# Attention weights turned in four tiles with another column order, a second score taken ahead, butterfly adds split over two engines, and PSUM pools in another order

## The chip, the cores and the metric

The kernel runs on one core of a Trainium2 chip. The core has five engines that work side by side, each through its own list of instructions in order: TensorE (PE, matrix products; its weight loads are shown apart as PEld), VectorE (DVE), ScalarE (ACT), GpSimd (POOL) and SyncE (SP, which here only issues DMA transfers). They meet through semaphores. The metric is the time of one execution on the device in microseconds (us); lower is better.

## The reference, cut to what matters

Everything is float32. The input is two images of 128 channels and 64 x 64 points. Layer 0 is a neighbourhood attention with its projections. Layer 1 takes the 4096 points of an image as tokens of 128 channels: a self-attention in which a token doesn't see itself, and then a "ffn" that filters along the tokens (a spectral convolution). The change is in layer 1.

```python
def _L1_attn_ref(q):                    # q: (2, 4096, 128), normalized tokens
    sim = jnp.einsum('blh,bmh->blm', q, q) * scale
    sim = jnp.where(diag[None, :, :], jnp.float32(-1000000000.0), sim)
    attn = jax.nn.softmax(sim, axis=-1)
    return jnp.einsum('blm,bmh->blh', attn, q)
...
x = x + _L0_conv_ref(_gn(x), ...)       # layer 0
t = _to_tokens(x)
t = t + _L1_attn_ref(_ln_t(t))          # layer 1: attention
t = t + _L1_ffn_ref(_ln_t(t), ...)      # layer 1: spectral filters
```

The filters are long convolutions over the tokens plus products with three short lags; the kernel computes the long ones with block transforms.

## The kernel before, in words

**Scores once for each pair.** Queries and keys are the same tokens, so the matrix of scores is symmetric. The 4096 tokens of an image are cut into 8 chunks of 512, and `attention(b, fill)` goes through the 36 pairs `(a, c)` with `c >= a`. For a pair and each of the four tiles `k` of 128 tokens of `a`, `weights` multiplies (L926; L935 for the diagonal pair `a == c` and for the pair (6, 7)) a tile of `a` with the 512 tokens of `c` into a PSUM `bank`, and ACT writes `exp` of it to SBUF, `e` (L931; L942 for the others). Four of them make the half `eh` of 128 x 2048.

**Each weight used twice.** `e` as it stands gives what the tokens of `a` add to the output of chunk `c`: four products `other <- e, tok` (L1056), summed in one PSUM bank, `other`, which DVE then adds to the output `xa` (L1065; L1067 is the copy for the first row). `other` has one buffer, so the next pair's first product waits until DVE has read it. Turned around, `e` gives what the tokens of `c` add to chunk `a`: products `own <- et, tok` (L984) into a bank that gathers a whole row `a`, added to `xa` at its end (L989, L991).

**Turning.** For pairs that are neither diagonal nor (6, 7) (`far`), `sent` writes `eh` to DRAM (`eb`, issued by ACT, L958), `moved` fetches it into `et` with the blocks of 32 rows exchanged (four DMAs from SP, L965), and `turned` turns the 32 x 32 blocks in place on DVE (L974). The other pairs are turned on PE (L948, L980, with copies L949 and L981 on DVE); in a diagonal pair DVE also masks the diagonal (L940), and tile `k` takes its columns left of the diagonal from the `exp` of earlier tiles, turned by PE. `MOVE, TURN, DELAY = 2, 7, 8` say how many steps after sending the fetch, the turning and the products are written down; one pair has four steps `j`. `pass_on(2)` puts up to two due turned products in the list, before the first `other` product of a pair and after each other one.

**What sets the order.** The inner loop writes for each step: one score of the following pair, due turned products, the product into `other`, and a piece of other work from `fill()`. That work comes from `filler`: layer norms and transforms of finished chunks (`after`), filters, weights of the ffn. In the beginning of the first image's attention a scheduler orders the instructions; from L1046 on the order is as written for PE, DVE, ACT, POOL and SP.

**The transforms' butterflies.** `after` ends with `store`: ACT copies a transform from PSUM to `uo` (L1156), and an addition and a subtraction of its halves go to `ub` (L1160), which is then sent to DRAM (`us`). `uo` has 2 buffers and `ub` 4. The engine is `adder[0]`: GpSimd in the attention, and DVE from the end of the second image's attention on (L1538). Then the DMAs to `us` are issued by SP (L1107), before that by GpSimd (L1091).

**The passage to the ffn.** After the attention the last chunks' `after` and the short lags (`short_lags`, products L1219, added to `xa` on DVE by L1235) remain. Then the attention's PSUM pools are closed, and the ffn opens its own: `ps_c` with four banks `pc` for the first products (L1597, copied to `y` by L1602), and `ps_p` with the sums `acc0` to `acc3` (L1616). The last short lags use these sums' banks too. The ffn fills the span's last 760 us, in an order written by hand for PE.

Of the kernel before, what the change touches and what calls it, by code (L numbers as in the profile page):

```python
# [9 lines left out]
AF = mybir.ActivationFunctionType  # L10
ALU = mybir.AluOpType
AX = mybir.AxisListType
PSUM = bass.MemoryType.PSUM

P = 128
# [13 lines left out]
ASCALE = P ** -0.5  # L29
# [73 lines left out]
def kernel(  # L103
# [16 lines left out]
    nc = tc.nc  # L120
# [18 lines left out]
    tt, tok, cm = [None, None], [None, None], [None, None]  # L139
# [6 lines left out]
    space = tok[0].rearrange("p n c -> p (n c)")  # L146
# [93 lines left out]
    with l0a:  # L240
# [64 lines left out]
        flat = rpb_pad.rearrange("h r w -> (h r w)")  # L305
# [384 lines left out]
        halves = [4 * c for c in CHUNKS]  # L690
# [101 lines left out]
        for k, (b, g) in enumerate(order):  # L792
            t = {}
# [83 lines left out]
    with ap_:  # L877
# [23 lines left out]
        def attention(b, fill):  # L901
# [11 lines left out]
            far = lambda a, c: a != c and (a, c) != (6, 7)  # L913
            chunk = lambda a: slice(CHUNKS[a] * 512, (CHUNKS[a] + 1) * 512)

            def weights(a, c, k, left, halves):

                n = 4 * CHUNKS[a] + k
                lo = k * P if a == c else 0
                ps = bank()  # L920
                if k == 0:
                    halves.append(ep.tile([P, 2048], F32, tag="e", name="e"))
                eh = halves[0]
                keys = cm[b][:, chunk(c)]
                if far(a, c):
                    nc.tensor.matmul(  # L926
                        ps.rearrange("p (q t j) -> p q t j", q=4, t=4), lhsT=cm[b][:, n * P : (n + 1) * P],
                        rhs=keys.rearrange("p (t q j) -> p q t j", t=4, q=4), start=True, stop=True,
                    )
                    e = eh.rearrange("p (q k r) -> p k q r", q=4, k=4)[:, k]  # L930
                    nc.scalar.activation(  # L931
                        e, ps.rearrange("p (q r) -> p q r", q=4), AF.Exp, bias=0.0, scale=ASCALE
                    )
                    return e
                nc.tensor.matmul(  # L935
                    ps[:, lo:], lhsT=cm[b][:, n * P : (n + 1) * P], rhs=keys[:, lo:], start=True, stop=True
                )
                if a == c:
                    ks = slice(k * P, (k + 1) * P)
                    nc.vector.tensor_tensor(ps[:, ks], ps[:, ks], ndiag, ALU.add)  # L940
                e = eh[:, k * 512 : (k + 1) * 512]
                nc.scalar.activation(  # L942
                    e[:, lo:], ps[:, lo:], AF.Exp, bias=0.0, scale=ASCALE
                )
                if lo:
                    pt = bank()
                    for j in range(k):
                        nc.tensor.transpose(pt[:, j * P : (j + 1) * P], left[j][:, lo : lo + P], ident)  # L948
                    nc.vector.tensor_copy(e[:, 0:lo], pt[:, 0:lo])  # L949
                return e  # L950

            def in_place(ins):
                return ins if ordered else tc.keep_in_program_order(ins)
# [15 lines left out]

            def turned(et):  # L970

                for q in (0, 2):
                    flat = et[:, q : q + 2].rearrange("p q r -> p (q r)")
                    in_place(nc.vector.transpose(flat, flat))  # L974

            def turned_here(et, es, m):

# [16 lines left out]
            def pair_onto(own, a, c, et, t):  # L994
                if (a, c) == (6, 7):
                    onto(own, 4 * CHUNKS[c] + t, own, et[:, t], False, t == 3)
                    if t == 3:
                        complete(a, own)
                    return
                onto(  # L1000
                    own, 4 * CHUNKS[c] + t, own.rearrange("p (k q i) -> p q k i", k=4, q=4),
                    et.rearrange("p q (k t i) -> p t q k i", k=4, t=4)[:, t], False, c == 7 and t == 3,
                )
                if (c, t) == (7, 3):
                    complete(a, own)

            coming_, late, turns, ordered, owns = [], [], [], [], {}
            step = 0

            def coming_of(a, c, k, left, halves):  # L1010

                e = weights(a, c, k, left, halves)
                if far(a, c) and k == 3:
                    coming_.append((step, sent(halves[0]), a, c))
                return e
# [16 lines left out]
            es, halves = [], []  # L1032
# [4 lines left out]
            for i, (a, c) in enumerate(pairs):  # L1037
                following = pairs[i + 1] if i + 1 < len(pairs) else None
                coming, halves = [], []
                if a != c:  # L1040
                    other = ps_o.tile([P, 512], F32, tag="other", name="other")
                else:
                    owns[a] = ps_o.tile([P, 512], F32, tag="own", name="own", bufs=2)
                for j in range(4):
                    if tt[1] is not None and not ordered:
                        ordered.append(written.enter_context(tc.manual_schedule(engines={engines.PE, engines.DVE, engines.Activation, engines.Pool, engines.SP})))  # L1046
                    if following:
                        coming.append(coming_of(*following, j, coming, halves))
                    n = 4 * CHUNKS[a] + j
                    turn = lambda v, o: v.rearrange(o, q=4) if far(a, c) else v  # L1050
                    if j == 0:
                        pass_on(2)
                    if a == c:
                        onto(owns[a], n, owns[a], es[j], j == 0, a == 7 and j == 3)
                    else:
                        nc.tensor.matmul(  # L1056
                            turn(other, "p (q r) -> p q r"), lhsT=tok[b][:, n, :], rhs=es[j],
                            start=(j == 0), stop=(j == 3),
                        )
                    if a != c and j == 3:  # L1060
                        xs, ov = xa[b][:, chunk(c)], other
                        if far(a, c):
                            xs, ov = xs.rearrange("p (t q j) -> p q t j", t=4, q=4), ov.rearrange("p (q t j) -> p q t j", q=4, t=4)
                        if a:
                            nc.vector.tensor_tensor(xs, ov, xs, ALU.add)  # L1065
                        else:
                            nc.vector.tensor_copy(xs, ov)  # L1067
                    if a != c and not far(a, c):
                        if j == 0:
                            here = ep.tile([P, 4, 512], F32, tag="et", name="et", bufs=2)  # L1070
                        turned_here(here, es, j)
                        late.append((step + 1, a, c, here, j))
                    if j:
                        pass_on(2)
                    fill()
                    step += 1
                es = coming
# [5 lines left out]
            written.close()  # L1083


        adder = [nc.gpsimd]
        queued_, turns_, crowd_ = [], [0, 0], [[]]

        def send_one():
# [26 lines left out]
        def after(b, c):  # L1116
# [35 lines left out]
            def store(pu, n, r0, m, ri):  # L1152

                for s in range(2):
                    both = sp.tile([P, 512], F32, tag="uo", name="uo", bufs=2)
                    nc.scalar.copy(both[:, 0 : 2 * n], pu[s][:, 0 : 2 * n])  # L1156
                    room()
                    ub = sp.tile([P, 2, 256], F32, tag="ub", name="ub", bufs=4)
                    for sgn, op in enumerate((ALU.add, ALU.subtract)):
                        adder[0].tensor_tensor(ub[:, sgn, 0:n], both[:, 0:n], both[:, n : 2 * n], op)  # L1160
                    to = us[b, par, r0 : r0 + m, :, :, 2 * hh + s, 2 * fp : 2 * fp + 2]
                    if ri is not None:
                        fresh(to[:, :, ri].rearrange("k g f d -> k g (f d)"), ub)
                        continue
                    for sgn in range(2):
                        for f in range(2):
                            fresh(to[:, sgn, :, f].rearrange("k i d -> i k d"), ub[64 * f : 64 * f + 64, sgn, 0:P])
# [17 lines left out]
            for e in range(2):  # L1185
                for f in range(2):
                    for s in range(2):
# [3 lines left out]
                            rhs=z[rows_, 2 * e + f, :], start=True, stop=True,  # L1191
# [343 lines left out]
        kept = []  # L1535
        fill, left = filler(1, steps, kept, slow)
        attention(1, fill)
        adder[:] = [nc.vector]  # L1538
        stores_left()
        crowd_[0] = None  # L1540
        for gen in (*steps, slow):
# [25 lines left out]
    outf = out.rearrange("b c h w -> b c (h w)")  # L1567
    with ExitStack() as cv:
        cp = cv.enter_context(tc.tile_pool(name="conv", bufs=5))
        ps_c = cv.enter_context(tc.tile_pool(name="ps_c", bufs=4, space=PSUM))  # L1570
        ps_p = cv.enter_context(tc.tile_pool(name="ps_p", bufs=1, space=PSUM))
        used = [0]

        def slot():
# [195 lines left out]
        b = NB - 1  # L1770
# [117 lines left out]
```

## Time and profile before

| | |
|---|---|
| median of 3 runs | 1981.72 us (1977.47 to 1988.21) |
| the profiled execution | 1969.95 us, its span from first to last instruction 1968.2 us |
| mean granted clock of TensorE | 0.992 |
| DVE transposes L974, 128x1024 | 108, mean 1220 ns |
| products L1056 (`other`), L984 (`own`, turned), L926 (scores), records | 448 of 595 ns, 448 of 596 ns, 432 of 599 ns |
| ACT `exp` L931, 128x512 | 216, mean 599 ns |
| butterflies L1160, 128x256 | 108 on POOL, mean 734 ns; on DVE median 418 ns over both sizes |

How to read it: the profile is of one execution on the chip. A row of the groups names line, engine, operation, what is written and read, the shape, the count, then busy time and mean length, then the idle time of the engine just before and who ended it. The ends of matmuls are modelled, so two that follow each other overlap in the record. Stages by time: layer 0 until about 350, attention of the first image to 750, of the second to 1145 (work of the neighbouring stages is mixed into each), the passage to 1210, the ffn to the end.

### The profile page before, as it was taken

The numbers are of one execution on the slowest core, as the hardware profiler recorded it, in microseconds if no ns is written. First come the engines' busy times: TensorE is split into PE (matmuls) and PEld (weight loads), VectorE is DVE, ScalarE is ACT, GpSimd is POOL, SyncE is SP. The second block draws the span as 40 slices with busy tenths as digits, with TensorE's granted clock in tenths as the row PEclk, the third lists the DMA queues.
The fourth block names the chain that finished last, engine by engine and source line by source line (L and its number), as shares of the span: only waits on it lengthen the run. The fifth ranks groups of instructions, "written<-read, shape, count | busy, mean of one in ns | idle before, by whom it ended". The sixth has DMA issues, their size and how long they took to land.

```text
span 1968.2 us, 50791 instructions
## 1 busy us (share of the span) xinstructions
PE 1897.2 (96%) x20504; PEld 1346.5 (68%) x20504; DVE 950.2 (48%) x2934; ACT 732.6 (37%) x1718; POOL 725.6 (37%) x1193
## 2 busy tenths in 40 slices
PE   6899998999999999999999998999999999999998
PEld 4577776444444444444444446999998999999987
DVE  5799997454554534354544374333333343333332
ACT  3789987323233333232332213222222222222221
POOL 4366886514633335533424420222221122222211
PEclk9999999999999999999999999999999999999999
DMA  5222221757766544988866413222222223222211
GB/s 155 63 62 61 62 61 39 178 158 227 219 185 191 151 121 126 260 214 231 242 191 184 126 46 84 69 66 68 66 66 54 58 74 86 67 66 68 67 39 44
DMA packets 249768, 226.14 MB, mean 115 GB/s; under 512 B 126815, under 2 KB 204655, under 8 KB 242112
## 3 DMA queue, kind: packets, MB, share of 16 engines
q1 hardware_dynamic: 222786, 129.15, 27.3%
q10 hardware_dynamic: 8126, 58.04, 7.6%
q0 software_dynamic: 18624, 35.72, 6.3%
q8 instruction: 163, 2.67, 0.6%
q14 instruction: 69, 0.57, 0.1%
HBM read 131.40 MB, written 91.25 MB: 113 GB/s over the span
## 4 chain that ended last, share of the span: by engine, by line
PE 82%; DVE 8%; POOL 4%; DMA 2%; issue 1%; ACT 1%; SPq 1%; ACTq 0%; DVEq 0%; POOLq 0%
PE acc L1616 28%; PE own L984 12%; PE bank L926 8%; PE other L1056 8%; PE pc L1597 7%; PE bank L349 2%; PE bank L935 2%; PE bank L559 2%; PE bank L1219 2%; PE bank L1175 2%; PE bank L202 2%; DVE et L974 1%; PE bank L523 1%; PE pc L1655 1%; PE po L581 1%
## 5 line engine op out<-in xcount | busy, mean ns | idle before, releaser
L1602 DVE COPY y<-pc 128x512 f32<-128x512 f32 x320 | 206.0, 685 | 346.7 <-PE pc L1597 346.4
L1616 PE MATMUL acc<-y,mpl 32*128 32x256 f32 x5120 | 323.1, 380 | 0.8 <-DVE af L1626 0.8
L1602 ACT COPY y<-pc 128x512 f32<-128x512 f32 x320 | 171.8, 589 | 393.3 <-PE pc L1597 388.1
L1616 PE MATMUL acc<-y,mmi 32*128 32x256 f32 x5120 | 315.1, 375 | 0.0
L1616 PEld LDWEIGHTS acc<-y,mpl 32*128 32x128 f32 x5120 | 289.0, 186 | 7.6 <-DVE af L1626 1.6
L1616 PEld LDWEIGHTS acc<-y,mmi 32*128 32x128 f32 x5120 | 290.7, 185 | 2.9
L1627 POOL TENSOR_TENSOR af<-af 128x512 f32<-128x512 f32 x39 | 49.8, 1276 | 597.5 <-DVE af L1626 597.5
L1056 PE MATMUL other<-e,tok 128*128 128x512 f32 x448 | 230.1, 595 | 6.8 <-DVE xa L1065 6.8
L931 ACT ACTIVATE e<-bank 128x512 f32<-128x512 f32 x216 | 129.2, 599 | 271.5 <-PE bank L926 264.4
L926 PE MATMUL bank<-cm 128*128 128x512 f32 x432 | 223.6, 599 | 0.0
L984 PE MATMUL own<-et,tok 128*128 128x512 f32 x448 | 212.1, 596 | 9.1 <-DVE et L974 4.7
L1597 PE MATMUL pc<-ct,ut 32*128 32x256 f32 x2560 | 210.1, 377 | 2.0 <-DVE y L1602 2.0
L1597 PEld LDWEIGHTS pc<-ct,ut 32*128 32x128 f32 x2560 | 171.5, 186 | 8.3 <-DVE y L1602 3.8
L984 PEld LDWEIGHTS own<-et,tok 128*128 128x128 f32 x448 | 83.2, 190 | 118.3 <-issue 93.7
L1160 POOL TENSOR_TENSOR ub<-uo 128x256 f32<-128x256 f32 (+1 forms) x160 | 99.2, 656 | 172.3 <-ACT uo L1156 153.6
L974 DVE STREAM_TRANSPOSE et<-et 128x1024 f32<-128x1024 f32 x108 | 127.7, 1220 | 57.6 <-DMA et<-eb 57.6
L1056 PEld LDWEIGHTS other<-e,tok 128*128 128x128 f32 x448 | 81.0, 190 | 100.5 <-issue 82.4
L926 PEld LDWEIGHTS bank<-cm 128*128 128x128 f32 x432 | 75.7, 190 | 72.8 <-issue 66.5
L546 ACT ACTIVATE p<-p,mn 128x196 f32<-128x196 f32 x256 | 114.4, 449 | 13.1 <-DVE mn L536 12.5
L1091 POOL DMA_DIRECT2D us<-ub x158 | 107.8, 723 | 11.5 <-DMA us<-ub 8.5
L1156 ACT COPY uo<-bank 128x512 f32<-128x512 f32 (+1 forms) x96 | 45.4, 517 | 98.3 <-PE bank L1175 57.8
L174 POOL TENSOR_TENSOR ln_rs<-ln_rs,mhalf 128x4 f32<-128x4 f32 x24 | 24.7, 1030 | 147.3 <-DVE ln_rs L173 147.3
(267 smaller groups left out, 2635.9 us busy)
## 6 DMA issues: line engine op xcount, KB each, us to landing
eb<-e ACTq DMA_DIRECT2D x54, 1024.0 KB
et<-eb SPq DMA_DIRECT2D x216, 256.0 KB
ut<-us SPq DMA_DIRECT2D x156, 128.0 KB
us<-ub POOLq DMA_DIRECT2D x54, 256.0 KB, 4.7
vw<-vd SPq DMA_DIRECT2D x256, 49.0 KB
ct<-gs SPq DMA_DIRECT2D x312, 40.0 KB
ct<-gs SPq DMA_DIRECT2D x312, 32.0 KB
vd<-v SPq DMA_DIRECT2D x128, 32.0 KB
```

The source lines that it names most:

```text
L546: nc.scalar.activation(p, p, AF.Exp, bias=t[name + "mn"][:, h : h + 1], scale=-1.0, accum_out=t["den"][:, u, h : h + 1],)
L926: nc.tensor.matmul(ps.rearrange("p (q t j) -> p q t j", q=4, t=4), lhsT=cm[b][:, n * P : (n + 1) * P], rhs=keys.rearrange("p (t q j) -> p ...
L931: nc.scalar.activation(e, ps.rearrange("p (q r) -> p q r", q=4), AF.Exp, bias=0.0, scale=ASCALE)
L974: in_place(nc.vector.transpose(flat, flat))
L984: nc.tensor.matmul(out_, lhsT=tok[b][:, n, :], rhs=e, start=first, stop=last, skip_group_check=True)
L1056: nc.tensor.matmul(turn(other, "p (q r) -> p q r"), lhsT=tok[b][:, n, :], rhs=es[j], start=(j == 0), stop=(j == 3),)
L1091: by.dma_start(out=to, in_=part)
L1160: adder[0].tensor_tensor(ub[:, sgn, 0:n], both[:, 0:n], both[:, n : 2 * n], op)
L1597: nc.tensor.matmul(pcs[j].rearrange("p (g o c) -> p o g c", g=4, o=2)[:, :, at], lhsT=ut[rows_, par, :], rhs=cv_[rows_], start=True, stop= ...
L1602: (nc.scalar.copy if j % 2 else nc.vector.tensor_copy)(y[:, :, :, 4 * kl + j, :], pcs[j].rearrange("p (g x k) -> p k g x", g=4, k=KF))
L1616: nc.tensor.matmul(acc[j][:, 0:256], lhsT=(mmi if l else mpl)[rows_, k, :], rhs=y[rows_, k, 2 * l : 2 * l + 2].rearrange("p s n x -> p (s ...
L1627: eng.tensor_tensor(af[:, 0:2], af[:, 0:2], af[:, 2:4], ALU.add)
```

## The change

Four parts:

1. `turned` makes four transposes, each of one tile `t` (4 x 128 columns of `et`), instead of two of 1024 columns in a row. For that the order of columns inside `eh` changes from (q, k, t, j) to (q, t, k, j), where `q` is the block of 32 rows, `k` the tile of `a`, `t` the tile of `c` and `j` the column in a block: ACT writes `e` so, `other` is read and written so, and `pair_onto` reads `et` so.
2. At the first step of a pair, if the pair isn't diagonal and no turned product is due, two scores of the following pair are put in the list instead of one; the second step then has none.
3. After the second image's attention only the subtractions of the butterflies go to DVE; the additions stay on GpSimd.
4. In the ffn the pool of the sums is opened before that of the first products, so that the sums get the first four banks.

```diff
-                    e = eh.rearrange("p (q k r) -> p k q r", q=4, k=4)[:, k]
+                    e = eh.rearrange("p (q t k j) -> p k q t j", q=4, t=4, k=4)[:, k]
                     nc.scalar.activation(
-                        e, ps.rearrange("p (q r) -> p q r", q=4), AF.Exp, bias=0.0, scale=ASCALE
+                        e, ps.rearrange("p (q t j) -> p q t j", q=4, t=4), AF.Exp, bias=0.0, scale=ASCALE
                     )
...
-                for q in (0, 2):
-                    flat = et[:, q : q + 2].rearrange("p q r -> p (q r)")
-                    in_place(nc.vector.transpose(flat, flat))
+                for t in range(4):
+                    part = et[:, :, t * P : (t + 1) * P]
+                    in_place(nc.vector.transpose(part, part))
...
-                    et.rearrange("p q (k t i) -> p t q k i", k=4, t=4)[:, t], False, c == 7 and t == 3,
+                    et.rearrange("p q (t k i) -> p t q k i", k=4, t=4)[:, t], False, c == 7 and t == 3,
...
-                    if following:
-                        coming.append(coming_of(*following, j, coming, halves))
+                    due = late and late[0][0] <= step
+                    while following and len(coming) < min(4, j + (2 if j == 0 and a != c and not due else 1)):
+                        coming.append(coming_of(*following, len(coming), coming, halves))
                     n = 4 * CHUNKS[a] + j
-                    turn = lambda v, o: v.rearrange(o, q=4) if far(a, c) else v
+                    turn = lambda v, o: v.rearrange(o, q=4, t=4) if far(a, c) else v
...
-                            turn(other, "p (q r) -> p q r"), lhsT=tok[b][:, n, :], rhs=es[j],
+                            turn(other, "p (q t j) -> p q t j"), lhsT=tok[b][:, n, :], rhs=es[j],
...
-        adder = [nc.gpsimd]
+        adder = [nc.gpsimd, nc.gpsimd]
...
                     for sgn, op in enumerate((ALU.add, ALU.subtract)):
-                        adder[0].tensor_tensor(ub[:, sgn, 0:n], both[:, 0:n], both[:, n : 2 * n], op)
+                        adder[sgn].tensor_tensor(ub[:, sgn, 0:n], both[:, 0:n], both[:, n : 2 * n], op)
...
         attention(1, fill)
-        adder[:] = [nc.vector]
+        adder[1] = nc.vector
...
+        ps_p = cv.enter_context(tc.tile_pool(name="ps_p", bufs=1, space=PSUM))
         ps_c = cv.enter_context(tc.tile_pool(name="ps_c", bufs=4, space=PSUM))
-        ps_p = cv.enter_context(tc.tile_pool(name="ps_p", bufs=1, space=PSUM))
```

## The prediction

> **What bounds the kernel now.** I read the page first, then the stretches of the span, then who TensorE waits for, and last the timeline around single waits.
>
> The page's first part, busy time by engine:
>
> ```profile
> span 1968.2 us, 50791 instructions
> ...
> PE 1897.2 (96%) x20504; PEld 1346.5 (68%) x20504; DVE 950.2 (48%) x2934; ACT 732.6 (37%) x1718; POOL 725.6 (37%) x1193
> ```
>
> TensorE (PE) is busy 96% of the span, so a change that gives it no less work can win only what it idles: 71 us in all. The stretches (length, then busy time of PE, PEld, DVE, ACT, POOL, granted clock, DMA share, GB/s) say how much of that lies where the diff reaches:
>
> ```profile
> 350.00:1150.00 800.00, 782.17 (x2507) 368.19 (x2506) 367.25 (x904) 245.25 (x463) 328.98 (x493) 1.00 0.66 184
> ...
> 1192.00:1194.00 2.00, 0.00 (x0) 0.00 (x0) 2.00 (x9) 0.00 (x0) 0.00 (x0) 1.00 0.47 149
> 1194.00:1198.00 4.00, 3.75 (x6) 1.50 (x6) 0.11 (x1) 0.00 (x0) 0.00 (x0) 0.65 0.14 43
> ```
>
> The two attention passes (350 to 1150) leave PE idle 17.8 us. DVE is 46% busy there (367.25 of 800). After it comes a hole before the first sums product at 1194, and a lower clock after it. What ends PE's waits in the attention (total, times, longest):
>
> ```profile
> PE other L1056 <- DVE xa L1065: 6.8, 10, 1.7
> PE own L984 <- DVE et L974: 4.7, 7, 1.0
> PE own L984 <- DVE et L981: 2.8, 2, 1.4
> ...
> PE own L984 <- POOL ub L1160: 1.0, 1, 1.0
> ...
> PE own L984 <- POOL tt L1507: 0.2, 1, 0.2
> ```
>
> Two kinds carry it: a product into `own` that waits for turned weights, and a first product into `other` that waits until DVE has read that bank. One of each in the timeline (start, length, what, and in brackets the idle time before):
>
> ```profile
> 580.80 2.36 DVE L974 STREAM_TRANSPOSE et<-et 128x1024 f32<-128x1024 f32 x2
> ...
> 581.62 1.02 PE L1056 MATMUL other<-e,tok 128*128 128x512 f32 x2
> ...
> 583.22 1.99 PE L984 MATMUL own<-et,tok 128*128 128x512 f32 x4 [0.57 <-DVE et L974]
> ```
>
> ```profile
> 1003.74 0.68 DVE L1065 TENSOR_TENSOR xa<-other,xa 128x512 f32<-128x512 f32 x1
> ...
> 1004.48 1.12 PE L1056 MATMUL other<-e,tok 128*128 128x512 f32 x2 [0.91 <-DVE xa L1065]
> ```
>
> One product is two matmul records (448 records for 224 products), 0.43 us apart from start to start and 0.59 long, so a product takes 0.86 us and a bracket of g means that PE is g + 0.16 us late.
>
> [...] and the row says 1220:
>
> ```profile
> L974 DVE STREAM_TRANSPOSE et<-et 128x1024 f32<-128x1024 f32 x108 | 127.7, 1220 | 57.6 <-DMA et<-eb 57.6
> ```
>
> [...] in the one place where the two share the butterfly of `uo` (four DVE adds beside GpSimd's, against four alone: 0.69 us more):
>
> ```profile
> 1149.12 2.12 DVE L1160 TENSOR_TENSOR ub<-uo 128x256 f32<-128x256 f32 x4 [3.17 <-ACT uo L1156]
> ...
> 1174.35 1.43 DVE L1160 TENSOR_TENSOR ub<-uo 128x256 f32<-128x256 f32 x4 [0.59 <-ACT uo L1156]
> ```
>
> [...] The stretch 1194 to 1198 shows it (0.65 granted) after 2.8 us of idleness.
>
> **The change, part by part**, against the profiled execution (span 1968.2, 1969.95 with what lies around it).
>
> *Turning tile by tile.* Before, two transposes cover all four tiles, so tile 0 is ready after 2.36 us. In the built program of the changed kernel each of the 216 `own` products waits for its own transpose. [...] bounds are half of the old one (0.61) and, if the four pieces of 128 columns cost as much as the whole did, 1.22. I take 0.69: tile 0 is ready 1.67 us earlier, tile 1 0.69 later, while PE needs 0.86 for a product. The nine waits of this kind (4.7 + 1.0 + 0.2 us idle, 0.99 the longest; the last two releasers are mere neighbours of a late L974) are 5.9 + 9 x 0.16 = 7.3 us of lateness, and three that show no idle time come 0.25 late: 8.1 us. All are shorter than 1.67, so all go. On DVE the four take 2.76 against 2.36 to 2.44, up to 0.4 us for each of 54 turns, 21 us at most: DVE has 433 idle us in these 800, so I cost it at nothing, except that an add queued behind a turn comes 0.4 us later. What follows a turn at 580 is statistics, which nobody on PE awaits.
>
> *Column order.* `exp` writes runs of 32 columns instead of 128, the product into `other` reads such runs, and the product into `own` reads runs of 128. Before, `own` read just these runs of 32, at 596 ns a record against 595 for `other`: no cost on PE. ACT's write could be slower; its row (216 of 599 ns) has 271 us of idle time before it, so even 0.1 us each is hidden. DMAs keep size and order; SP's list is unchanged.
>
> *Second score ahead.* It moves one score (0.86 us, no new work) in front of the first `other` product in pairs without a due turned product. Of the ten waits on L1065, seven stand right behind a lone score: idle 0.37, 0.50, 0.37, 0.91, 0.90, 0.91, 0.38, lateness 0.16 more each. The cover takes 0.53, 0.66, 0.53, 0.86, 0.86, 0.86, 0.54 = 4.8 us. Two (at 708 and 1102) stand before a diagonal pair: there the second score drags along a transpose of the first score's `exp`, which ends at about 1102.5 when `other` was free at 1101.7; the stall is exchanged for another, +0.15 us each, +0.3 in all. The tenth (509, 1.74 idle) has due products ahead and stays. The banks that the early scores take are free by older `exp`s.
>
> *Adds on GpSimd, subtracts on DVE after the attention.* 16 adds go to GpSimd at 0.73 us (0.50 for 128 columns), where DVE took 0.42 (0.28). Side by side a pair would need 0.73 instead of 0.84; [...] Until 1188 the stores' SP queue is behind anyway and hides it. At the end, from 1190.2, three pairs run to the last DVE add before the sums: 2.0 us before, between 1.6 and 2.7 now. -0.2 to +0.9; I take +0.3, with some overlap.
>
> *Sums' banks first.* The hole at 1194 is a wait of the first sums product for the last L1235, which reads another bank. The built program moves that product to a bank that had been free for long, yet it still lists the same wait, the last L1235 (L1236 now): the new pool waits for everything that the old one held. So the 2.8 us and the half clock (six matmuls in 4.5 us instead of 2.7) stay: nothing.
>
> Sum: -8.1 - 4.8 + 0.3 + 0.3 = -12.3. I give back a tenth, 1.3 us, for PE arriving earlier at DVE's other releases with DVE's turns 0.4 longer: **-11.0 us**, a span of 1957.2. The median shown, 1981.72, is 11.8 us over the profiled execution; I carry the difference over unchanged: **1970.7 us**.
>
> **Rivals.**
> (a) *The waits come back elsewhere*: DVE's longer turns stand in front of L1065, L1067 and L989, and each add 0.4 us late for 20 to 25 pairs takes 8 to 10 us back. For it: these adds do end PE waits. Against: most have a due product in front. Time about 1979.
> (b) *More is gained than the profile shows*: runs without the profiler take 11.8 us more, and if that is partly such waits, the cover takes more; the same if the sums' wait ends early after all (2.8 + 1.8 us). Time about 1963.
> (c) *Slower*: the transpose of four separate pieces is paid like the whole, 1.22 us each. Then tile t is ready at 1.22(t+1) while PE takes a product each 0.86: each later tile falls 0.36 us behind, up to 1.08 for a turn, or 58 us for 54 turns if all came due without slack; and DVE gains 54 x 2.4 = 130 us of work, which delays the `other` adds. With slack in half of the turns, 29 - 12 = +17 us: 1999. It decides from about 0.9 us for one transpose. Against: the elements are the same and each piece is 128 contiguous columns.
>
> **How the numbers follow.** A measurement of this kernel tells about 0.5% (10 us) from no change. Forecast 60%, and in three quarters of it the gain passes 10 us; (b) 16%; (a) 14%; (c) 10%. Faster 0.45 + 0.16, rounded to 0.61; same 0.15 + 0.14 = 0.29; slower 0.10. The range reaches past (b) to 1960 and past (a) to 1983, leaving out (c); the likeliest case alone spans 1966 to 1975.
>
> **What would show it.** L974 at about 0.69 us in four; no PE wait on L974; PE waits on the `other` add down from 6.8 to about 2.5 us; two new waits L948 <- L942 near 700 and 1090; the sums product still 2 to 4 us behind L1236, with a half-clock window; GpSimd and DVE butterfly pairs over 0.84 us. It is wrong if transposes take over 0.9 us, if `other` waits grow, or if the hole at 1194 is gone.

## The result, and the profile after

The changed kernel takes 1964.29 us (median of 7 runs, 1962.27 to 1969.45); beside it the kernel before takes 1980.21 us (7 runs, 1972.14 to 1988.21). The ratio is 0.9928, with a 95% interval of 0.9911 to 0.9944: some 14 us less, between 11 and 18. The forecast was 1970.7 us, in a range of 1960 to 1983, and "faster". Direction and range held; the time lies under the 1966 to 1975 that the likeliest case was given, and the gain is larger than the 11 us of the sum.

The profiled execution took 1964.29 us, its span 1962.6 us. The page's first part:

```profile
span 1962.6 us, 50908 instructions
...
PE 1898.9 (97%) x20504; PEld 1351.1 (69%) x20504; DVE 955.2 (49%) x3026; ACT 732.2 (37%) x1718; POOL 737.7 (38%) x1209
```

TensorE has the same 20504 matmul records as before, so all of the gain must be idle time or clock. The two attention passes as one stretch (length, then busy time of PE, PEld, DVE, ACT, POOL, granted clock, DMA share, GB/s):

```profile
350.00:1150.00 800.00, 788.02 (x2548) 374.27 (x2549) 380.54 (x1035) 247.44 (x468) 335.28 (x500) 1.00 0.66 186
```

PE idles 12.0 us of these 800 where it idled 17.8. The waits behind that (total, times, longest) from 345 to 1150:

```profile
PE own L984 <- DVE et L974: 3.4, 2, 3.0
PE own L984 <- DVE et L981: 2.8, 2, 1.4
PE bank L948 <- ACT e L942: 2.3, 5, 0.6
PE other L1057 <- DVE xa L1066: 2.2, 1, 2.2
```

(Lines behind L1047 stand one lower in the changed file: L1057 is L1056 of before, L1066 is L1065, L1161 is L1160, L1220 is L1219, L1236 is L1235.) Both kinds that carried the sum have shrunk: waits on the add into `xa` from 6.8 us in ten to 2.2 in one, and waits on the turning from seven to two. One of these two is 3.0 us long, longer than any of its kind in the profile before. The group of the transposes:

```profile
L974 DVE STREAM_TRANSPOSE et<-et 128x512 f32<-128x512 f32 x216 | 134.2, 679 | 75.9 <-DMA et<-eb 75.8
```

And the two places that the prediction showed, in the timeline after:

```profile
581.27 2.48 DVE L974 STREAM_TRANSPOSE et<-et 128x512 f32<-128x512 f32 x4
...
582.09 1.02 PE L1057 MATMUL other<-e,tok 128*128 128x512 f32 x2
...
582.95 1.88 PE L984 MATMUL own<-et,tok 128*128 128x512 f32 x4
```

```profile
1000.61 0.68 DVE L1066 TENSOR_TENSOR xa<-other,xa 128x512 f32<-128x512 f32 x1
...
1001.35 1.98 PE L1057 MATMUL other<-e,tok 128*128 128x512 f32 x4
```

In the first, the product into `own` starts 1.68 us after the first transpose, while the last transposes still run, and has no idle time before it (0.57 before). In the second, the product into `other` stands behind two scores and no longer waits for the add (0.91 before).

**By stages the two first profiles do not add up to the runs.** The attention here is measured from the start of the first product into `own` to that of the last one; the passage reaches to the first product of the ffn's sums (L1616), and the next stage to the last of them. Worked out from the start times in each trace (us):

| profile | until the attention | attention | passage | sums of the ffn | behind them | span |
|---|---|---|---|---|---|---|
| before | 350.3 | 794.3 | 66.2 | 739.3 | 18.2 | 1968.2 |
| after | 352.7 | 785.9 | 66.4 | 739.3 | 18.2 | 1962.6 |

The profiles differ by 5.6 us, the medians by 16. The profiled execution of before lay 11.8 us under the median of its first three runs (10.3 under the 1980.21 above); that of after is its own median. So the first question was what an ordinary execution of the kernel before looks like, and the second which part of the change takes it away.

### The profile page after: what moved, and what is told of

It reads as the page before. It is cut to its first block, busy times and chain, and to the rows that moved or that the text cites. A ratio compares the mean times of both kernels' runs of the same rounds, so it can differ in the third digit from the quotient of the medians.

```text
span 1962.6 us, 50908 instructions
## 1 busy us (share of the span) xinstructions
PE 1898.9 (97%) x20504; PEld 1351.1 (69%) x20504; DVE 955.2 (49%) x3026; ACT 732.2 (37%) x1718; POOL 737.7 (38%) x1209
## 4 chain that ended last, share of the span: by engine, by line
PE 79%; DVE 6%; POOL 5%; DMA 4%; issue 2%; ACT 2%; SPq 1%; DVEq 0%; POOLq 0%; ACTq 0%
PE acc L1617 29%; PE own L984 11%; PE bank L926 8%; PE other L1057 8%; PE pc L1598 7%; PE bank L349 2%; PE bank L935 2%; PE bank L202 2%; PE bank L559 1%; PE bank L1176 1%; PE bank L1220 1%; DMA et<-eb 1%; ACT p L546 1%; DMA us<-ub 1%; DMA eb<-e 1%
## 5 line engine op out<-in xcount | busy, mean ns | idle before, releaser
L1057 PE MATMUL other<-e,tok 128*128 128x512 f32 x448 | 227.5, 594 | 2.3 <-DVE xa L1066 2.2
L931 ACT ACTIVATE e<-bank 128x512 f32<-128x512 f32 x216 | 129.2, 599 | 250.6 <-PE bank L926 246.3
L1161 POOL TENSOR_TENSOR ub<-uo 128x256 f32<-128x256 f32 (+1 forms) x176 | 111.5, 668 | 178.8 <-ACT uo L1157 150.8
L974 DVE STREAM_TRANSPOSE et<-et 128x512 f32<-128x512 f32 x216 | 134.2, 679 | 75.9 <-DMA et<-eb 75.8
L1057 PEld LDWEIGHTS other<-e,tok 128*128 128x128 f32 x448 | 81.4, 191 | 92.1 <-issue 82.4
L546 ACT ACTIVATE p<-p,mn 128x196 f32<-128x196 f32 x256 | 114.4, 449 | 14.4 <-DVE mn L536 13.7
L536 DVE CUSTOM_DVE_ANT_0 p<-bank,tab 128x196 f32<-128x196 f32 x256 | 76.5, 354 | 4.9 <-PE bank L523 4.7
```

The costliest lines, as they stand in the source:

```text
L536: nc.vector.tensor_tensor_reduce(t[name + "p"][:, h, :], t[name + "S"][h][:, 0:KEYS], tab[:, ci, h, :], 1.0, 3.0e38, ALU.add, ALU.min, t[n ...
L546: nc.scalar.activation(p, p, AF.Exp, bias=t[name + "mn"][:, h : h + 1], scale=-1.0, accum_out=t["den"][:, u, h : h + 1],)
L931: nc.scalar.activation(e, ps.rearrange("p (q t j) -> p q t j", q=4, t=4), AF.Exp, bias=0.0, scale=ASCALE)
L974: in_place(nc.vector.transpose(part, part))
L1057: nc.tensor.matmul(turn(other, "p (q t j) -> p q t j"), lhsT=tok[b][:, n, :], rhs=es[j], start=(j == 0), stop=(j == 3),)
L1161: adder[sgn].tensor_tensor(ub[:, sgn, 0:n], both[:, 0:n], both[:, n : 2 * n], op)
```

## Experiments

The theory: *the finer turning carries the gain.* It takes away the near misses that the profile before shows, and it also shortens a stall that this profile happened to lack, so that the turning is worth more than 8.1 us. The rivals: the second score ahead gives its 4.5 us besides; the column order or the split of the butterflies does something of its own; the missing 12 us lie elsewhere in the run.

### The parts, one by one

*Turning and column order alone*, on the kernel before:

```diff
+                    e = eh.rearrange("p (q t k j) -> p k q t j", q=4, t=4, k=4)[:, k]
...
-                for q in (0, 2):
-                    flat = et[:, q : q + 2].rearrange("p q r -> p (q r)")
-                    in_place(nc.vector.transpose(flat, flat))
+                for t in range(4):
+                    part = et[:, :, t * P : (t + 1) * P]
+                    in_place(nc.vector.transpose(part, part))
```

> Before plus the turning tile by tile and its column order, nothing else. My theory (nine waits on L974 and three late products go, 8.1 us): the time from the first product into own to the last product into other falls from 784 us to about 776, no wait on L974 over 0.5 us except where the fetched weights land late, the ten waits on L1065 (6.8 us) stay; ratio to before 0.993 to 0.996. Rival 'longer turns push the adds': that time falls by less than 4 us and the waits on L1065 grow past 9 us; ratio 0.998 to 1.000.

*The second score ahead alone*, on the kernel before:

```diff
-                    if following:
-                        coming.append(coming_of(*following, j, coming, halves))
+                    due = late and late[0][0] <= step
+                    while following and len(coming) < min(4, j + (2 if j == 0 and a != c and not due else 1)):
+                        coming.append(coming_of(*following, len(coming), coming, halves))
```

> Before plus the second score ahead, nothing else. My theory (4.8 us of cover, 0.3 given back at two diagonal pairs): the time from the first product into own to the last product into other falls from 784 us to about 779.5, waits on L1065 from 6.8 to about 2.5 us, waits on L974 stay near 4.7; ratio to before 0.996 to 0.998. Rival 'the score was needed where it stood': new waits of PE for exp or for banks eat it, ratio 0.999 to 1.001.

*The changed kernel with two transposes of 1024 columns*, over the new column order:

```diff
-                for t in range(4):
-                    part = et[:, :, t * P : (t + 1) * P]
-                    in_place(nc.vector.transpose(part, part))
+                for q in (0, 2):
+                    flat = et[:, q : q + 2].rearrange("p q r -> p (q r)")
+                    in_place(nc.vector.transpose(flat, flat))
```

> After, but with the two transposes of 1024 columns each in the new column order. My theory: each own product waits again for both, so eight or nine waits on L974 of 0.6 to 1 us come back, and the attention is 5 to 8 us longer than with four; ratio to before 0.995 to 0.998. Rival 'the column order, not the finer turning, is what helps': ratio as after, 0.992 to 0.994.

*The changed kernel with the late butterflies wholly on DVE*, as before:

```diff
-        adder[1] = nc.vector
+        adder[:] = [nc.vector, nc.vector]
```

> After, but all butterflies after the attention on DVE as before. My theory ([...]+0.3 us): the time from the last product into other to the first sums product of the ffn loop changes by less than 1 us from the 76.7 of after, ratio to before equal to after's 0.9928 within 0.001. Rival 'the split carries the gain outside the profile': ratio 0.996 or more.

All four ran beside the same runs of the kernel before (1979.57 us median, 45 runs):

| | median us | ratio to before (95%) | attention in its profile |
|---|---|---|---|
| turning and column order alone | 1964.94 | 0.9930 (0.9906 to 0.9954) | 790.6 |
| second score alone | 1975.45 | 0.9993 (0.9980 to 1.0006) | 797.7 |
| all but the finer turning | 1974.44 | 0.9981 (0.9969 to 0.9992) | 798.5 |
| all, late butterflies on DVE | 1962.96 | 0.9919 (0.9893 to 0.9946) | 791.6 |

The turning alone (with the column order that it needs) gives the whole gain within its interval. Without it 4 us (2 to 6) are left, from column order, score, split and banks together. The split makes no difference that these runs can tell. (A ratio here is worked out from all the runs, with its interval, and isn't that of the medians: those of the second score and of before lie 4.1 us apart, the ratio says 1.4.) The ratios of the turning and of the split are as expected. That of the second score alone is its rival's (0.999 to 1.001), and that of all but the finer turning lies just above the expected 0.995 to 0.998.

The expectations measure the attention to the last product into `other`, 784.6 us in the first profile. So measured it is 780.9 us with the turning alone (776 expected) and 788.0 with the second score alone (779.5 expected): in single profiles neither part showed what it was to save, and the reason follows.

But the waits do not look as the sum had them. The waits of PE in the attention with the turning alone, then with all but the finer turning:

```profile
PE other L1056 <- DVE xa L1065: 7.3, 10, 2.2
PE own L984 <- DVE et L974: 3.0, 2, 2.6
```

```profile
PE own L984 <- DVE et L974: 9.6, 8, 5.4
...
PE other L1057 <- DVE xa L1066: 2.8, 1, 2.8
PE bank L948 <- ACT e L942: 2.1, 4, 0.6
```

Each part does remove its own kind of wait: the turning leaves two on L974, the score one on the add. The new thing is one long wait on the turning, 2.6 us here and 5.4 there. It stands near 915 to 927 in each of the four, as in the profile after, where the timeline says what it waits for:

```profile
913.54 2.49 DVE L974 STREAM_TRANSPOSE et<-et 128x512 f32<-128x512 f32 x4 [4.01 <-DMA et<-eb]
...
914.30 2.40 PE L984 MATMUL own<-et,tok 128*128 128x512 f32 x4 [3.02 <-DVE et L974]
```

DVE itself stood idle for 4.01 us until the fetched weights landed, and PE waited for 3.02. Two transposes of 1024 columns would have kept it some 1.7 us longer (2.37 us for both of them, against 0.68 for the first of four).

### An ordinary execution of the kernel before

The kernel before, unchanged, profiled again.

> The kernel before, unchanged, profiled a second time. Theory 1 (the first profile was an unusually quick execution: 1968.2 us of span where 45 runs have a median of 1979.6, and it is the only one of six profiles without a late landing of fetched weights at 900 to 950): the span is 1974 to 1982, with a wait of PE on L974 of 3 to 6 us near 915 and a half-clock window of 3.4 us after it, and the sum of the waits on L974 grows from 4.7 to 8 to 12 us. Theory 2 (the missing 10 us lie all over the run and not in the attention): the first own product to the last other product again takes about 784 us, and the difference shows in other stages.

It took 1980.08 us; the 31 runs of this kernel beside it have a median of 1979.64. The span is 1978.4 us, 10.2 us longer than in the first profile, and the attention took 801.1 us, 6.8 longer. Waits of PE in the attention, and the place that the first profile did not have:

```profile
PE other L1056 <- DVE xa L1065: 7.5, 10, 2.4
PE own L984 <- DVE et L974: 7.3, 6, 4.0
```

```profile
921.34 2.37 DVE L974 STREAM_TRANSPOSE et<-et 128x1024 f32<-128x1024 f32 x2 [3.35 <-DMA et<-eb]
...
923.76 3.68 PE L984 MATMUL own<-et,tok 128*128 128x512 f32 x4 [4.02 <-DVE et L974]
```

The fetch lands at 921.3, the two transposes take 2.37 us, and only then, after 4.02 us, does PE go on. It goes on slowly: four matmuls in 3.68 us instead of 1.88. The stretch right behind the wait, with the granted clock, the DMA share (a transfer counts whole where it begins, so a short stretch can pass 1) and GB/s as the last three figures:

```profile
924.00:928.00 4.00, 4.00 (x6) 1.60 (x6) 2.90 (x6) 0.28 (x1) 0.75 (x1) 0.59 1.04 230
```

So theory 1 of this run holds for two thirds of the difference: 6.8 of 10.2 us are in the attention: 4.0 us of waiting at 924 where the first profile had 0.6, and two half-clock windows of 3.4 us (behind this wait and at 511), each of which costs 1.7 us (twelve short-lag matmuls that meet such a window in the profile after, at 1181.92, take 7.11 us, and twelve at 1186.04 in the first profile, without one, 5.42). The rest is 1.3 us before the attention and 2.0 in the passage, where one more half-clock window of 3.4 us falls (at 1210.6). The wait sum of 7.3 us just missed the 8 to 12 expected. The first profile is the unusual one: of the 45 runs that stood beside the first four experiments only one was shorter than its 1969.95 us.

Against this second profile the turning alone has an attention of 790.6 instead of 801.1 us: 10.5 less; against the first it is 3.7. The pair that differs by the finer turning and nothing else, all but the finer turning and the change, gives 12.6 (798.5 to 785.9).

### More time between the landing and the products

If what counts is the time from the landing to the first product, a later product should help like finer turning. One line sets it:

```diff
-MOVE, TURN, DELAY = 2, 7, 8
+MOVE, TURN, DELAY = 2, 9, 10
```

It was put into the kernel with the second score alone, and into the changed kernel with the late butterflies on DVE.

> The kernel before with the second score ahead, and with the turning and the turned products written down two steps later (TURN, DELAY = 9, 10 for 7, 8), so that a fetch has two more steps, some 5 us, to land; the turning still is two transposes of 1024 columns and still stands one step before its products. Theory 1 (late landings cost the wait near 915 and the clock after it): this wait, 4.8 us with the second score alone, is gone or under 1 us, 1.7 us of half clock go with it, and the median falls by 5 to 8 us from 1975.4 to about 1969. The small waits on two transposes (about 3.6 us) stay. Rival (the cost is only that of two transposes that take 2.4 us in front of the first product, wherever they stand): no change, 1973 to 1977.

> The changed kernel with the later butterflies wholly on DVE, and with two more steps for the fetches to land (TURN, DELAY = 9, 10). Theory 1: the one wait on L974 left (4.9 us near 915 in the profile with the later butterflies on DVE) and its half clock go, the median falls from 1963.0 to about 1957, under both kernels. Rival: the fetch is held up by the two et buffers, which are freed two steps later too, so that nothing changes (1961 to 1965); or the later completion of rows makes the passage to the ffn longer by up to 5 us.

Both kernels got slower: 1983.43 us (ratio 1.0023, 1.0012 to 1.0034) and 1968.53 us (0.9949, 0.9932 to 0.9966), where neither theory nor rival had put them. The slack itself did come. With the second score DVE waits for landings 23.8 us in the attention instead of 67.7, the late landing that had cost PE 4.82 us isn't waited for any more, and no half-clock window is left there, as theory 1 had it. But new waits came, in the first kernel and in the second:

```profile
PE bank L948 <- ACT e L942: 13.7, 17, 2.0
PE own L984 <- DVE et L974: 11.6, 14, 2.9
```

```profile
PE bank L948 <- ACT e L942: 14.5, 17, 2.7
PE own L984 <- DVE et L974: 1.6, 1, 1.6
```

For the transposes of diagonal pairs (L948 on L942) PE had waited 2.3 and 2.1 us without the edit. And with the second score the first product now comes 2.7 us (median) behind the first transpose of its weights, where it was 4.2; why was not followed further. A part of the two steps is also given back. There are two `et` buffers, and in these traces no fetch goes out before the last product that reads its buffer has ended: in the first kernel 27 of 52 go out within 0.1 us behind that end (5 without the edit), and the median from sending to fetch is 9.7 us instead of 5.9. So a fetch takes no buffer too early here either, against what the expectation for the next edit says of 9 and 10.

One thing makes these two kernels unfit for use: in the program as built the shift lets one block of the ffn's filters (`negatives`) be overwritten before its store is issued. The attention has the same products, on the same weights, as without the edit, so its waits can be read. As a pair the two differ, apart from the sums' banks and the column order, by the transposes alone: where the product follows right behind the turning, fourteen waits on L974 became one, and the median fell by 14.9 us.

The next edit moves one step only: the fetch is taken three steps after sending, the turning stays, the products come at nine. That is one step more from turning to product, but from fetch to product it is six steps as before.

```diff
-MOVE, TURN, DELAY = 2, 7, 8
+MOVE, TURN, DELAY = 3, 7, 9
```

> The kernel before, with its two transposes of 1024 columns, and one constant line changed: fetch three steps after sending, turn seven, products nine (MOVE, TURN, DELAY = 3, 7, 9 for 2, 7, 8), so that turning has two steps before its products instead of one. Unlike with 9 and 10, a fetch never takes the buffer of a pair whose products are still to come. Theory 1 (the gain is the time between the landing and the first product): the near misses of 0.5 to 1 us on L974 go without any finer turning, the late one near 915 falls from 4.0 to under 2 us, and the median falls from 1979.6 to 1966 to 1972; what finer turning gains (some 11 to 14 us), another step of slack gains too. Rival (finer transposes also help in a way of their own, such as a lighter load on DVE or SBUF): 1976 to 1980. Second rival: DVE blocks on a late fetch in front of the add into xa, so that the waits on L1065 grow from 7 to over 10 us and eat the gain.

> The changed kernel with the later butterflies wholly on DVE, and the same three constants (3, 7, 9). Theory 1: only the late landing near 915 is left to gain there, 3 to 5 us of wait and 1.7 us of half clock, of which the step takes up to 2.5 us and the clock: 1957 to 1961, against 1963.0 without it. Rival: products that come a step later meet the adds and the copies of diagonal pairs (L948 on L942) at another moment, as in the runs with 9 and 10, where those waits grew by 11 us: 1964 to 1975.

On the kernel before: 1969.12 us (ratio 0.9965, 0.9946 to 0.9983, beside 1977.7 us of before in that session). The median is inside the expected 1966 to 1972, though the ratio makes it a gain of 7 us, where the turning gave 14. The waits:

```profile
PE bank L948 <- ACT e L942: 3.7, 4, 1.5
PE own L984 <- DVE et L981: 2.6, 2, 1.3
PE other L1056 <- DVE xa L1065: 2.5, 11, 0.6
...
PE own L984 <- DVE et L974: 1.0, 2, 0.6
```

Two transposes of 1024 columns with a step more in front of the products wait for 1.0 us in all instead of 7.3; the late one near 915 and its half clock are gone. For the near misses that is the step's work. For the late one it is not shown: there the transposes begin 9.9 us after the last transfer of the fetch went out, where it was 13.0 in the second profile of before and 9.0 in the first, so in this execution the weights came early. The second rival (DVE blocks in front of the add) is out: the waits on the add fell too, from 7.5 us to 2.5; why was not followed further. The transposes of diagonal pairs lose 2.4 us (L948 on L942: 3.7, and 1.3 in the first profile). So a step more and finer turning remove the same near misses, and the step did not gain as much. In the plain times the intervals (0.9946 to 0.9983, and 0.9906 to 0.9954 for the turning) still overlap.

On the changed kernel the same line gives 1963.15 us (0.9923, 0.9900 to 0.9945), where it is 0.9919 without: no gain, between the theory's 1957 to 1961 and the rival's 1964 to 1975. L974 no longer stands among PE's waits at all, but L948 on L942 rose from 2.1 to 5.1 us. Of the 4.9 us that the late landing had cost, 3.0 came back there.

### The second score once more

The changed kernel with the late butterflies on DVE, with one score at each step:

```diff
-                    while following and len(coming) < min(4, j + (2 if j == 0 and a != c and not due else 1)):
+                    while following and len(coming) < min(4, j + 1):
```

> The changed kernel with the later butterflies wholly on DVE and without the second score ahead: finer turning, the column order and the sums' banks first. Theory 1 (the second score takes 4.5 us off the attention): the stage from the first own product to the last other product is 780 us instead of 776, and the median is 1965 to 1969 against 1963.0. Rival (the time taken off the attention is waited for again behind it, on the way to the ffn): the attention is 4 us longer but the whole is 1961 to 1964.

1966.65 us, ratio 0.9939 (0.9920 to 0.9957), against 0.9919 (0.9893 to 0.9946) with the second score. Its waits beside those of the kernel that differs by the second score alone, first without it, then with it:

```profile
PE other L1057 <- DVE xa L1066: 7.8, 10, 2.7
...
PE own L984 <- DVE et L974: 2.3, 1, 2.3
```

```profile
PE own L984 <- DVE et L974: 4.9, 1, 4.9
PE other L1057 <- DVE xa L1066: 3.6, 1, 3.6
...
PE bank L948 <- ACT e L942: 2.1, 4, 0.6
```

Nine waits on the add are gone (-4.2 us), as foreseen; the late landing is waited for 2.6 us longer and the diagonal pairs 1.2 us (L948 on L942 was 0.9). The median is the theory's (1965 to 1969), but neither theory's stage came out: the attention is 791.1 us without and 791.6 with the second score. In plain times the three pairs of runs say 1.4 us for the second score (from 0.9993), 0.4 (0.9930 and 0.9928) and 4.0 (0.9939 and 0.9919), each uncertain by 3 us or more.

The clock hides the rest. In these two profiles the half-clock windows in the attention add up to 6.8 us without and 13.7 with the second score. Taken out, the parts come close to adding up. For the runs, each run's span times its granted clock (both on record) estimates the span at full clock, as far as TensorE is the limit; for the profiles it is the attention less half of the half-clock time in it. In us, the runs against before beside them, with a 95% interval from resampling the runs:

| | span x clock | attention | half clock in it | attention at full clock |
|---|---|---|---|---|
| before, first and second profile | 0 | 794.3, 801.1 | 0, 6.8 | 794.3, 797.7 |
| turning and column order alone | -10.9 (-12.5 to -9.6) | 790.6 | 3.4 | 788.9 |
| second score alone | -3.5 (-4.7 to -2.4) | 797.7 | 6.8 | 794.3 |
| all but the finer turning | -4.2 (-5.5 to -2.8) | 798.5 | 10.2 | 793.4 |
| the change | | 785.9 | 3.4 | 784.2 |
| all, late butterflies on DVE | -15.0 (-16.7 to -13.4) | 791.6 | 13.7 | 784.8 |
| the same without the second score | -9.2 (-10.6 to -7.7) | 791.1 | 6.8 | 787.7 |
| before with fetch, turning, products at 3, 7, 9 | -5.5 (-7.2 to -3.8) | 792.6 | 0 | 792.6 |

At full clock the second score is worth 3.5 us alone and 5.8 beside the finer turning (9.2 to 15.0), and the turning some three times as much as the second score. The step more gives half of the turning's gain, and there the intervals don't meet. In clock the runs of the turning alone lost 3.1 us less (0.8 to 5.2) than before, those of the second score alone 1.8 more (0.1 to 3.6). Whether these parts cause that was not tested.

## Why the prediction was right, and where its sum was off

**Turning tile by tile: right in kind, the size too small.** A transpose of 512 columns takes 679 ns, four in a row 2.48 us. The 0.69 taken (2.76 for four) was the author's estimate between the bounds of 0.61 and 1.22. An estimate from the profile before alone gives the same: on a straight line between DVE's 0.42 us for an add of 256 columns and its 1.22 for a transpose of 1024, 512 columns take 0.69. Tile 0 is ready early enough that the near misses go: of seven waits in the first profile and six in the second, two are left with the turning alone. Rival (c), 1.22 us for each, is out. The term was -8.1 us, and it is the step of the sum that was mis-sized. Measured: -14 (-9 to -19) in the runs, -10.9 at full clock, and -8.8 (797.7 to 788.9) and -9.2 (793.4 to 784.2) in the attentions at full clock. Two things were left out. One is the late landing at 915 to 925, which the profile that the sum was read from does not have, while the seven other profiles with `MOVE, TURN, DELAY` at 2, 7, 8 all have it (2.3 to 5.4 us of waiting). There the first of four transposes lets PE go on some 1.65 us earlier (0.76 or 0.77 us from the first transpose to the product, 2.41 before), which makes 8.1 some 9.8; the prediction's "so all go" was true of the waits in its view only. The other is the clock: every wait was priced at full clock, and the runs lost 3.1 us less to half clock.

**Column order: nothing, as said.** Products keep 594 and 595 ns a record, and `exp` its median of 597 ns (L931). No run changed it alone.

**Second score: the mechanism as said, the gain in plain times too large.** The waits on the add fell to 2.2 us (about 2.5 was named), the tenth stayed, and the two waits of L948 on L942 at diagonal pairs appeared (0.57 us each, at 706 and 1097). The -4.5 us became -1.4 (-4.0 to +1.2) alone on the kernel before, but -3.5 (-4.7 to -2.4) at full clock. So the cover of "0.53, 0.66, 0.53, 0.86, ..." was nearly right, and what is lacking is mostly clock, which the sum priced for one window only, that at 1194. PE also comes earlier to the late landing and in the three pairs of profiles waited longer there, by 0.8, 2.6 and 0.4 us; as that landing differs between executions of one kernel too, it isn't shown that the second score causes this.

**Split of the butterflies: within its bounds.** +0.3 (-0.2 to +0.9) was taken, an estimate of the author's. The passage is 66.4 us after and 64.9 with these adds on DVE, 66.2 and 68.2 in the profiles before; the runs cannot tell the two apart. What the split does is plain in the timeline:

```profile
1179.96 0.43 DVE L1161 TENSOR_TENSOR ub<-uo 128x256 f32<-128x256 f32 x1 [2.46 <-DMA us<-ub]
1180.00 0.97 POOL L1161 TENSOR_TENSOR ub<-uo 128x256 f32<-128x256 f32 x1 [1.91 <-DMA us<-ub]
1181.00 0.37 ACT L1157 COPY uo<-bank 128x256 f32<-128x256 f32 x1 [2.30 <-POOL ub L1161]
...
1181.43 0.65 PE L202 MATMUL bank<-ident,tt 128*128 128x128 f32 x4 [2.02 <-ACT uo L1157]
...
1190.34 2.81 PE L1220 MATMUL acc<-tt,mu 128*128 128x512 f32 x6 [1.31 <-DVE xa L1236]
```

GpSimd's add, which itself stood 1.91 us behind a store, holds `uo`, ACT's copy waits for it, and PE's transposes for the copy: a hole of 2.02 us, and the half-clock window comes here (0.50 granted from 1182.0 to 1185.4). The sums' first product then waits for 1.31 us instead of 2.80. The idle time has moved forward, and the passage has not become shorter.

**Sums' banks first: nothing, as said.** The first sums product still ends its wait on the last L1236, in the bank order of the change too: 1.31 us above, and 2.4 us with the butterflies on DVE, against 2.80 and 1.3 in the two profiles before. The named sign "2 to 4 us behind L1236" so did not show in the profile after, and the half-clock window, in the first profile behind this wait (0.50 granted from 1195.2 to 1198.5), came ahead of it. No run changed this edit alone.

**The sum and its starting point.** -11.0 us were foreseen and -14.3 (-11 to -18) came. The likeliest case names the right mechanism, with its main term mis-sized. Of the 6.4 us between forecast and time, 1.5 come from the kernel before, which took 1980.21 us beside the change where the forecast began from 1981.72. The 11.8 us carried over were taken for something that runs have and profiles lack; they are the distance of one execution from the median. Rival (b), "runs without the profiler take 11.8 us more, and if that is partly such waits, the cover takes more" (1963), names what happened more closely and has the nearer number; only its word "profiler" is wrong, since a second profile shows these waits. That the range held owes something to its being stretched to cover (b). Rival (a), waits that come back behind DVE's longer turns, did not come: with the turning alone the waits on the add were 7.3 us, between the 6.8 and 7.5 of the two profiles before.

**No version clearly beats the change.** The late butterflies wholly on DVE (0.9919) and the same with one step more (0.9923) lie inside the interval of the change (0.9911 to 0.9944).

## What to carry to other kernels

Before a sum is made against one profile, ask where that execution stands among the runs: this one lay a dozen us under the median, and it lacked a stall and two half-clock windows that its second profile has. Where runs differ in granted clock, compare them at full clock too: here that brought out a gain of 3.5 us for the second score, where the plain ratio couldn't tell one from none. Where a consumer takes its data in pieces, let the producer finish them in pieces too: the gain is not only the near misses seen, but also whatever lateness of the transfer in front still comes. And before a delay is written into a schedule with rotating buffers, count when each buffer comes free for the next fetch, and what else moves with it.

## What had not been expected of the hardware

- The landing of 1 MB of weights beside other traffic is not the same from one execution to the next: with the same program DVE could begin to turn them 13.0 us after the last transfer went out in one profile, and PE waited 4.02 us near 924, while at that turn in the other they lay ready after at most 9.0 us and PE waited 0.57 us for the transposes alone. The DMA share from 900 to 924 doesn't tell the two apart: 0.87 and 0.86.
- A DVE subtract and a GpSimd add of 256 columns that start 0.04 us apart take 1.01 us together (0.43 for the first, 0.97 for the second). Alone and four in a row, DVE's start every 0.34 us (1.43 us for four of 0.42) and GpSimd's every 0.68 (2.77 us for four of 0.72, at 1147.07 in the profile before), 1.02 in sum. So in this pair they take side by side what they take one after the other. Where the two start together in the profile before, at 1149.12, it is DVE's add that gets longer, 1.00 us for 0.42, and GpSimd's takes its 0.72. What holds one of them back, the traces do not show. The upper bound of the split, 0.73 + 0.42 = 1.15 for a pair, added up lengths, whose ends overlap where such instructions follow each other (0.42 long, 0.34 from start to start).
- A wait of 4.0 us near 924 was followed by a half-clock window of 3.4 us, and so was one of 2.4 us at 511 in the same profile, while one of 2.56 us at 511 in the profile with the second score alone was not. What decides it, these runs do not show.
